# A recommender's attention over history: three gathers in 256 replaced by single-row DMAs from ScalarE's and SyncE's queues

## The chip, the cores and the metric

The kernel runs on one core of one Trainium2 chip. The metric is the device time of one execution in microseconds (us); lower is better. It is given as the median of several runs of the same program. One more execution is recorded by the hardware profiler; every row of a profile below comes from that one.

## The reference

For 16384 samples and a history of 200 items each, the reference looks up embedding rows of 64 floats, scores each history item against the sample's own item with a small two-layer network, sums the history with these scores, and passes the result through a head of three layers.

```python
it = i_emb[item]
h = i_emb[hist]                                   # 200 x 16384 rows of 64 floats
itb = jnp.broadcast_to(it[None], h.shape)
feat = jnp.concatenate([h, itb, h - itb, h * itb], axis=-1)
a = dice(feat @ au_W1 + au_b1, au_alpha, axis=1)  # mean and variance over the samples
w = a @ au_W2 + au_b2
cur = jnp.sum(w * jax.lax.stop_gradient(h), axis=0)
z = jnp.concatenate([u, it, c, cur], axis=-1)
z = dice(z @ W1 + b1, alpha1, axis=0)
z = dice(z @ W2 + b2, alpha2, axis=0)
return z @ W3 + b3
```

`dice(x)` is `x * (p + alpha * (1 - p))` with `p = sigmoid((x - mean) / sqrt(var + eps))`.

## The kernel before

**Setup.** A table in DRAM is built first: for every item its 64 floats and 64 more that are the part of the first layer that depends on the history item alone, 512 bytes a row. Meanwhile rows of item, user and category are gathered for the samples themselves. Then the head's weights are loaded (`load_head_weights`, L175), many small DMAs on SyncE's (SP's) queue.

**Main loop.** A step `k` handles 2048 history items: history row `k // 8`, chunk `k % 8` of the samples. A chunk is 16 tiles of 128 rows. There are 1600 steps: 7 turns of a hardware loop of 192 steps (24 history rows, L498) and 256 steps written out after it. Each step (`step`, L438) does a piece of several steps' work:

- `fetch(k)` (L366): GpSimd (POOL) issues 16 indirect DMAs (`gather`, L199, the instruction on L202), one for each tile; each fetches 128 table rows, one to a partition, into the buffer `land[k % 12]`. SP then loads `xit`, the part of the first layer that depends on the sample's item (L369).
- ScalarE (ACT) evaluates the sigmoid of step k-10 (L448) and scales it (L451), into the PSUM tile `pg`.
- VectorE (DVE) transposes step k-1's rows (`turn`, L377) into `hx`; ACT copies half of it to `ph` (L454); DVE adds the hidden layer of step k-2 (L390) and takes its statistics (L392); ACT copies `xit` to `px` (L458); DVE multiplies by the sample's item (L384) and TensorE (PE) adds the product's layer (L240).
- Once in 8 steps `moments` (L417) turns a history row's statistics into factors for the sigmoid; ACT takes the square root (L249).
- DVE weighs step k-10 (`weigh`, L396: L398 to L415) and adds it to `cur`.

`land` has 12 buffers. A buffer is used by a gather at step k, by the transpose at step k+1 and by `weigh` at step k+10, so POOL may run up to two steps ahead of DVE. The order inside an engine is the order written in `step`: the scheduler is switched off in this part.

**Synchronisation.** Each DMA sent from SP's or ACT's queue counts up one of eight semaphores, taken in turn in program order over both queues; a DMA waits until the earlier one on its semaphore has landed. POOL's DMAs have eight of their own.

**Head.** The last 10 steps are mixed with the first layer of the head (`layer1`, L527). Then come the factors of its normalisation (`row_factors`, L544), and for each of 8 chunks `dice` (L560: ACT L563, DVE L564 and L565), the second layer on PE (L593), the copy with bias by ACT (L595) and the sums by DVE (`row_sums`, L525). The third layer and the output follow.

Of the kernel before, what the change touches and what calls it, by code (L numbers as in the profile page):

```python
# [8 lines left out]
F32 = mybir.dt.float32  # L9
I32 = mybir.dt.int32  # L10
AF = mybir.ActivationFunctionType
# [3 lines left out]
P = 128  # L15
D = 64
# [3 lines left out]
CD = 2 * CH  # L20
LPB = 24
LAND = 12
EARLY = 4
IDX = 2
XI = 2
# [3 lines left out]
def din_kernel(  # L29
# [24 lines left out]
    nc = tc.nc  # L54
    L, B = r_hist.shape
    NT = B // P
# [51 lines left out]
    for g in range(2):  # L108
# [14 lines left out]

    land = [const.tile([P, TD, 2 * D], F32, name=f"land{i}") for i in range(EARLY)]
    idx = [const.tile([P, NT], I32, name=f"idx{i}") for i in range(IDX)]
    stats = [const.tile([P, 2 * ND, nc.vector.BN_STATS_DIM], F32, name=f"st{i}") for i in range(2)]
    rstds = [const.tile([P, 1], F32, name=f"rs{i}") for i in range(2)]
    shifts = [const.tile([P, 1], F32, name=f"sh{i}") for i in range(2)]
# [12 lines left out]
    J = P // (2 * ZB)  # L141
    w1a = const.tile([P, 4, P], F32, name="w1a")
    w1b = const.tile([P, 4, P + 2 * ZB * (J - 1)], F32, name="w1b")
    w2a = const.tile([P, 2 * Z2], F32, name="w2a")
    w2b = const.tile([P, J, 2 * Z2], F32, name="w2b")
    w3 = const.tile([2 * Z2, (2 * ND - 1) * 2 * ZO], F32, name="w3")

    za, zb, z2 = (
        [const.tile([n, 1], F32, name=f"{m}{i}") for i in ("b", "al", "1al")]
# [4 lines left out]
    mean_of = {  # L154
        n: const.tile([n * m, n * m], F32, name=f"mean{n}") for n, m in ((ZA, 2), (ZB, 2 * J), (Z2, 2))
    }
    zstats = [
        const.tile([n, m, nc.vector.BN_STATS_DIM], F32, name=f"zst{i}")
        for i, (n, m) in enumerate(((P, 2 * ND), (P, 2 * ND // J), (2 * Z2, 2 * ND)))
    ]  # L160
    zbase = dram.tile([ND + ND // J, P, CD], F32, name="zbase")

    for n, t in mean_of.items():
# [9 lines left out]
        nc.vector.tensor_scalar_mul(t, ph[: n * m, : n * m], 1.0 / m)  # L173

    def load_head_weights():  # L175
        for t in (w1a, w1b, w2a, w2b, w3):
            nc.vector.memset(t, 0.0)  # L177
        for g in range(2):
            for e in range(2):
                rows = W1.rearrange("(f d) z -> d f z", d=D)[e * S : (e + 1) * S]  # L180
                nc.sync.dma_start(w1a[quarter(e, g), :, ts(g, ZA)], rows[:, :, :ZA])
                z0 = 2 * ZB * (J - 1) + ZB * g
                nc.sync.dma_start(w1b[quarter(e, g), :, z0 : z0 + ZB], rows[:, :, ZA:])
            nc.sync.dma_start(w2a[ts(g, ZA), ts(g, Z2)], W2[:ZA])
            for j in range(J):
                nc.sync.dma_start(w2b[ts(2 * j + g, ZB), j, ts(g, Z2)], W2[ZA:])
            o0 = (ND - 1) * 2 * ZO + ZO * g
            nc.sync.dma_start(w3[ts(g, Z2), o0 : o0 + ZO], W3)
        nc.sync.dma_start(bias3, b3.partition_broadcast(S))
        for i, (v, w) in enumerate(((b1, b2), (alpha1, alpha2))):  # L190
            for g in range(2):
                nc.sync.dma_start(za[i][ts(g, ZA)], col(v)[:ZA])
                nc.sync.dma_start(z2[i][ts(g, Z2)], col(w))
            for m in range(2 * J):
                nc.sync.dma_start(zb[i][ts(m, ZB)], col(v)[ZA:])
        for t in (za, zb, z2):
            nc.vector.tensor_scalar(t[2], t[1], -1.0, 1.0, ALU.mult, ALU.add)

    def gather(dst, ids, rows):  # L199

        for n in range(ids.shape[1]):
            nc.gpsimd.indirect_dma_start(  # L202
                out=dst[:, n, :],
                out_offset=None,
                in_=rows,
                in_offset=bass.IndirectOffsetOnAxis(ap=ids[:, n : n + 1], axis=0),
            )
# [3 lines left out]

    def load_hist_ids(i, l):
        nc.sync.dma_start(idx[i], r_hist[ds(l, 1), :].rearrange("l (p n) -> p (l n)", n=NT))

    def by_tile(t, i):

# [118 lines left out]
    with ExitStack() as main:  # L335
# [19 lines left out]
        for i in range(2):  # L355
            nc.vector.memset(rstds[i], 0.0)
            nc.vector.memset(shifts[i], 0.0)
        nc.sync.dma_start(xit[-1 % XI], xi[ND - 1])

        def by_row(t):  # L360
            return t.rearrange("p (n d) -> p n d", d=D)
# [3 lines left out]

        def fetch(k):  # L366
            l, c = divmod(k, ND)
            gather(land[k % LAND], idx[l % IDX][:, ts(c, TD)], table)
            nc.sync.dma_start(xit[k % XI], xi[c])  # L369

        def turn(k):

# [65 lines left out]
        def step(k, last=None):  # L438


            def has(j):
                return last is None or j <= last

            if has(k):
                fetch(k)
            if has(k - 10):
                i = (k - 10) // ND % 2
                nc.scalar.activation(  # L448
                    by_row(pg), x_of(k - 10), AF.Sigmoid, bias=shifts[i], scale=rstds[i]
                )  # L450
                nc.scalar.activation(pg, pg, AF.Identity, bias=au_al, scale=au_1al)  # L451
            if has(k - 1):
                turn(k - 1)
                nc.scalar.copy(ph, hx[(k - 1) % 2][:, 0])  # L454
            if has(k - 2):
                hidden(k - 2)
            if has(k - 1):
                nc.scalar.copy(px, xit[(k - 1) % XI])  # L458
                product(k - 1)
            if has(k - 2) and (k - 2) % ND == ND - 1:  # L460
                moments((k - 2) // ND)
            if has(k - 10):
                weigh(k - 10)

        def fetch_ids(k, l0, n):
            l, c = divmod(k, ND)
            if c == 0 and l + 1 < n:
                load_hist_ids((l + 1) % IDX, l0 + l + 1)

        def window(j):  # L470
            return slice(2 * ZB * (J - 1 - j), 2 * ZB * (J - 1 - j) + P)

        def base_of_layer1():

            for rest in (False, True):
                for c in range(ND):
# [12 lines left out]
                    if last:  # L489
# [4 lines left out]
                        yield  # L494
                        yield

        rest_l = L % LPB + LPB
        with tc.For_i(0, L - rest_l, LPB) as l0:  # L498
            with tc.manual_schedule():
                for k in range(LPB * ND):  # L500
                    fetch_ids(k, l0, LPB + 1)
                    step(k)


# [11 lines left out]
        def rest_of(c):  # L516
            return home(homes[ND + c // J])
# [5 lines left out]
        def row_sums(i, n, m, t):  # L523
            for h in range(2):
                nc.vector.bn_stats(zstats[i][:, 2 * m + h, :], t[:n, ts(h, CH)])  # L525
# [34 lines left out]
        def dice(dst, t, p, factors, consts):  # L560
# [3 lines left out]
            nc.vector.tensor_scalar(p[:n], p[:n], consts[2], consts[1], ALU.mult, ALU.add)  # L564
            nc.vector.tensor_mul(dst[:n], p[:n], t)  # L565

        with tc.manual_schedule():
            work = base_of_layer1()
            for k in range(K):
                fetch_ids(k, L - rest_l, rest_l)  # L570
                step(k, last=K - 1)
                next(work, None)
            load_base(0, 1)
            for k in range(K, K + 10):
                step(k, last=K - 1)
                if k < K + 4:
                    load_base(*((2, 3), (ND, ND + 1), (4, 5), (6, 7))[k - K])
                c = k - K - 2
                if c >= 1:
                    keep1(c - 1)  # L580
                if c >= 0:
                    layer1(c)
            keep1(ND - 1)

            spare = [home(i) for i in range(18, 24)]
            fa, fb = row_factors(0, ZA, P), row_factors(1, ZB, P)
            for c in range(ND):
                if c % J == 0:
                    dice(rest_of(c), rest_of(c), spare[4 + c // J], fb, zb)
                a = spare[c % 4]  # L590
                dice(a, z_of(c), a, fa, za)
                po = (px, pz, pg, ph)[c % 4]
                layer(po[: 2 * Z2], [(w2a, a), (w2b[:, c % J], rest_of(c))])  # L593
                t = home(10 + c)[: 2 * Z2]
                nc.scalar.activation(t, po[: 2 * Z2], AF.Identity, bias=z2[0])  # L595
                row_sums(2, 2 * Z2, c, t)
            f2 = row_factors(2, Z2, 2 * Z2)
            n = ND * 2 * ZO
            for c in range(ND):
                a = spare[c % 4]  # L600
                dice(a, home(10 + c)[: 2 * Z2], a, f2, z2)
                at = (ND - 1 - c) * 2 * ZO
                for i in range(2):
                    nc.tensor.matmul(  # L604
                        px[:n, ts(i, CH)], w3[:, at : at + n], a[: 2 * Z2, ts(i, CH)],
                        start=(c == 0), stop=(c == ND - 1),
                    )
# [45 lines left out]
```

## Time and profile before

| What | Value |
|---|---|
| Timed runs, median of 3 | 36744.62 us (36743.43 to 36755.11) |
| Profiled execution | 32783.09 us |
| its span, first to last instruction | 32780.9 us |
| granted TensorE clock, mean | 0.547 of full speed |
| POOL gathers from the table, L202 | 25600, mean 943 ns |
| all POOL indirect DMAs | 25984 |
| DVE busy | 25567.4 us (78%) |
| ACT busy | 7755.2 us (24%) |
| DMA moved over the span | 2667.86 MB, 1214773 packets, 81 GB/s |

The profiled execution is shorter than the timed runs by 12%, so a duration from a row belongs to the profiled execution, and a sum of rows is to be set against its time. In a row of costly groups stand the line, the engine, the operation with its output and inputs, the count, then busy time in us and mean ns of one, then the engine's idle time just ahead of these instructions and what ended most of it; "issue" means that the engine waited for nothing that the profile shows. In a row of the timeline stand the start and the duration in us, and in brackets the idle time ahead and its releaser. SPq and ACTq are the queues on which these engines send DMAs.

### The profile page before, as it was taken

What the parts mean: (1) busy time and instruction counts of PE and PEld (TensorE: products, weight loads), DVE (VectorE), ACT (ScalarE), POOL (GpSimd) and SP (SyncE); (2) the same over time, 40 slices, a digit from 0 to 9 for tenths busy, and PEclk for the clock granted to TensorE, in tenths of its full rate; (3) what the DMA queues carried; (4) which work ended last, traced back from release to release, by engine and by line L of the source; (5) the groups of instructions that cost most, each with busy time, mean ns of one, the idle gap of its engine ahead of it and who ended that gap; (6) DMA issues with size and microseconds to landing.
All of it is one profiled execution on the core that took longest, in us unless ns stands there. A gap on an engine that the chain in (4) does not pass through costs nothing. (4 is left out here: it accounts for less than half of the span.)

```text
span 32780.9 us, 100656 instructions
## 1 busy us (share of the span) xinstructions
PE 6366.6 (19%) x7006; PEld 2038.0 (6%) x7006; DVE 25567.4 (78%) x28797; ACT 7755.2 (24%) x7105; POOL 24515.6 (75%) x25991
## 2 busy tenths in 40 slices
PE   3111111111111111111111111111111112221112
PEld 0000000000000000000000000000000000000000
DVE  7777777777777777777777777777777777777777
ACT  1222222222222222222222222222222222222222
POOL 7777777777777777777777777777777777777775
PEclk5555555555555555555555555555555555555555
DMA  5222222222222222222222222222222223332222
GB/s 157 80 79 79 79 79 79 79 79 79 79 80 80 79 78 79 79 79 80 79 79 79 79 79 78 79 79 80 78 79 79 79 79 85 88 90 81 79 79 60
DMA packets 1214773, 2667.86 MB, mean 81 GB/s; under 512 B 551244, under 2 KB 577388, under 8 KB 1207916
## 3 DMA queue, kind: packets, MB, share of 16 engines
q0 software_dynamic: 831488, 1691.97, 19.6%
q1 hardware_dynamic: 372012, 906.09, 9.1%
q10 hardware_dynamic: 10560, 63.79, 0.5%
q14 instruction: 692, 5.67, 0.1%
q8 instruction: 21, 0.34, 0.0%
HBM read 2590.90 MB, written 69.16 MB: 81 GB/s over the span
## 5 line engine op out<-in xcount | busy, mean ns | idle before, releaser
L202 POOL DMA_INDIRECT land<-table,idx x25600 | 24152.2, 943 | 7872.6 <-issue 7703.8
L377 DVE STREAM_TRANSPOSE hx<-land 64x1024 f32<-64x1024 f32 x6404 | 7938.2, 1240 | 6360.3 <-DMA land<-table,idx 6218.5
L240 PE MATMUL px<-hx,blk_m 128*128 128x512 f32 x6408 | 5927.6, 1080 | 26007.0 <-DVE hx L384 25941.1
L448 ACT ACTIVATE pg<-land,sh,rs 128x1024 f32<-128x1024 f32 x1610 | 1943.8, 1207 | 12980.0 <-DVE cur L415 11593.3
L454 ACT COPY ph<-hx 128x1024 f32<-128x1024 f32 x1601 | 1627.6, 1017 | 10365.2 <-DVE hx L377 10362.2
L240 PEld LDWEIGHTS px<-hx,blk_m 128*128 128x128 f32 x6408 | 1880.1, 324 | 30022.8 <-issue 29846.4
L392 DVE BATCH_NORM_STATS2 st<-land 128x6 f32<-128x512 f32 x3204 | 2060.9, 685 | 55.0
L400 DVE STREAM_TRANSPOSE hx<-pg 128x1024 f32<-128x1024 f32 x1610 | 2011.7, 1250 | 55.2
L414 DVE TENSOR_TENSOR pg<-land,ph 128x1024 f32<-128x1024 f32 x1610 | 1977.8, 1228 | 55.0
L415 DVE TENSOR_TENSOR cur<-pg,cur 128x1024 f32<-128x1024 f32 x1610 | 1970.5, 1224 | 55.6
L402 DVE TENSOR_REDUCE r<-hx 128x32 f32<-128x1024 f32 x1610 | 1964.0, 1220 | 55.3
L390 DVE TENSOR_TENSOR land<-px,hx 128x1024 f32<-128x1024 f32 x1602 | 1961.6, 1224 | 49.5
L398 DVE TENSOR_TENSOR pg<-pg,land 128x1024 f32<-128x1024 f32 x1610 | 1968.8, 1223 | 2.7 <-ACT pg L451 2.5
L384 DVE TENSOR_TENSOR hx<-ph,itT 128x1024 f32<-128x1024 f32 x1601 | 1932.0, 1207 | 0.0
L451 ACT ACTIVATE pg<-pg,au_al,au_1al 128x1024 f32<-128x1024 f32 x1610 | 1895.0, 1177 | 54.3
L458 ACT COPY px<-xit 128x1024 f32<-128x1024 f32 x1601 | 1627.2, 1016 | 383.3 <-DVE land L390 381.1
L409 DVE SCALAR_TENSOR_TENSOR ph<-r,au_bias,r 64x16 f32<-64x16 f32 x3220 | 771.3, 240 | 114.8
L406 DVE COPY r<-r 64x32 f32<-64x32 f32 x1610 | 337.2, 209 | 55.0
L448 ACT ACT_TABLE_LOAD x209 | 268.1, 1283 | 452.6 <-DVE w1a L177 314.6
L249 ACT ACT_TABLE_LOAD x203 | 260.4, 1283 | 6.7 <-PE ph L555 3.2
L249 ACT ACTIVATE std<-var,eps 128x1 f32<-128x1 f32 x201 | 59.2, 295 | 475.2 <-DVE var L435 475.2
L425 DVE COPY other<-mv 32x2 f32<-32x2 f32 x804 | 155.6, 194 | 15.1
(122 smaller groups left out, 1885.8 us busy)
## 6 DMA issues: line engine op xcount, KB each, us to landing
xit<-xi SPq DMA_DIRECT2D x1601, 512.0 KB
land<-table,idx POOLq DMA_INDIRECT x25600
table<-tab ACTq DMA_DIRECT2D x48, 1024.0 KB
tab<-in_L_rec_i_emb SPq DMA_DIRECT2D x48, 512.0 KB
zt<-ucT SPq DMA_DIRECT2D x32, 512.0 KB
idx<-in_r_hist SPq DMA_DIRECT2D x200, 64.0 KB
ucT<-t ACTq DMA_DIRECT2D x16, 512.0 KB
zbase<-zt SPq DMA_DIRECT2D x10, 512.0 KB
```

The source lines that it names most:

```text
L202: nc.gpsimd.indirect_dma_start(out=dst[:, n, :], out_offset=None, in_=rows, in_offset=bass.IndirectOffsetOnAxis(ap=ids[:, n : n + 1], axis=0),
L240: nc.tensor.matmul(dst[:, cols], lhsT, rhs[:, cols], start=(j == 0 and not onto), stop=(j == len(pairs) - 1), skip_group_check=onto,)
L377: nc.vector.transpose(dst.rearrange("p s (n t) -> p n s t", t=S), rows[ts(i, D), :, :, e])
L384: nc.vector.tensor_mul(hm, ph, itT[:, k % ND])
L390: nc.vector.tensor_add(x_of(k), by_row(px), by_row(hx[k % 2][:, 1]))
L392: nc.vector.bn_stats(stats[l % 2][:, 2 * c + i, :], x_of(k)[:, ts(i, TD // 2)])
L398: nc.vector.tensor_mul(by_row(pg), by_row(pg), x_of(k))
L400: nc.vector.transpose(yT, pg)
L402: nc.vector.tensor_reduce(r, yT.rearrange("p (i n u) -> p i n u", i=2, u=S), mybir.AxisListType.X, ALU.add)
L414: nc.vector.tensor_mul(by_row(pg), rows, w.unsqueeze(2).to_broadcast([P, TD, D]))
L415: nc.vector.tensor_add(cur[:, ts(c, TD)], by_row(pg), cur[:, ts(c, TD)])
L448: nc.scalar.activation(by_row(pg), x_of(k - 10), AF.Sigmoid, bias=shifts[i], scale=rstds[i])
```

## The change

Every eighth step (k % 8 = 7) and every sixteenth (k % 16 = 11) the last of the 16 tiles is no longer gathered by POOL. Its 128 rows are fetched by 128 plain DMAs of one row each, whose source address is read from a register: for the first kind from ACT's queue, 16 in each of the 8 steps before, for the second from SP's queue, 8 in each of the 16 steps before. They go into a buffer of their own (`side`, two of each kind), and ACT copies it into `land` at the step concerned. The addresses are loaded from the history by SP six steps before the first row is sent, multiplied by 512 by DVE four steps before, and read into registers (16 or 8 at once) in each step ahead of its DMAs. Part of these DMAs is sent before the loop starts.

The load of `xit` moves from `fetch`, at the head of the step, to behind ACT's second copy and SP's and ACT's row DMAs. To make room in memory the weights of the head's second and third layers and the head's statistics live in `zt`, a buffer that is free by then, and are loaded 16 steps before the end. In the head, chunk c's copy and sums (`keep2`) come after the matmuls of chunk c+2 have been issued.

```diff
+SIDES = ((8, 7), (16, 11))
+EARLIER = 0
+ROW = 4 * 2 * D
...
+    side = [[const.tile([P, 2 * D], F32, name=f"side{q}{i}") for i in range(2)] for q in range(2)]
+    addr = [[const.tile([1, P], I32, name=f"addr{q}{i}") for i in range(2)] for q in range(2)]
...
+    def load_addresses(q, m, l):
+
+        n = SIDES[q][1] % ND * TD + TD - 1
+        ids = r_hist[ds(l, 1), :].rearrange("l (p n) -> l n p", n=NT)[:, n : n + 1]
+        with nc.allow_non_contiguous_dma(reason="one index of each partition"):
+            nc.sync.dma_start(addr[q][m % 2].unsqueeze(1), ids)
+
+    def to_addresses(q, m):
+
+        nc.vector.tensor_scalar_mul(addr[q][m % 2], addr[q][m % 2], ROW)
+
+    def side_of(k):
+
+        for q, (every, at) in enumerate(SIDES):
+            if k % every == at:
+                return q, k // every
+        return None
...
+        flat = table.rearrange("v d -> (v d)").bitcast(U8)
+
+        queues = ((nc.scalar, mybir.EngineType.Activation), (nc.sync, mybir.EngineType.SP))
+
+        def rows_by_address(q, m, part):
+
+            dst = side[q][m % 2].bitcast(U8)
+            n = P // SIDES[q][0]
+            engine, kind = queues[q]
+            _, at = nc.values_load_multi_w_load_instructions(
+                addr[q][m % 2][:, ts(part, n)],
+                engines=(kind,), min_val=0, max_val=ROW * (V - 1),
+                skip_runtime_bounds_check_because="the DMA checks the address against the table",
+            )
+            for j, a in enumerate(at):
+                p = part * n + j
+                engine.dma_start(dst[p : p + 1], flat[ds(a, ROW)].rearrange("(o d) -> o d", o=1))
...
         def fetch(k):
             l, c = divmod(k, ND)
-            gather(land[k % LAND], idx[l % IDX][:, ts(c, TD)], table)
-            nc.sync.dma_start(xit[k % XI], xi[c])
+            n = TD - (side_of(k) is not None)
+            gather(land[k % LAND][:, :n], idx[l % IDX][:, c * TD : c * TD + n], table)
...
                 moments((k - 2) // ND)
+            if has(k):
+                if side_of(k):
+                    q, m = side_of(k)
+                    nc.scalar.copy(land[k % LAND][:, TD - 1], side[q][m % 2])
+                for q in (1, 0):
+                    every, at = SIDES[q]
+
+                    m, part = divmod(k + every + EARLIER - at, every)
+                    if has(m * every + at):
+                        rows_by_address(q, m, part)
+                nc.sync.dma_start(xit[k % XI], xi[k % ND])
             if has(k - 10):
                 weigh(k - 10)
...
+        for q, (every, at) in enumerate(SIDES):
+            done = divmod(every + EARLIER - at, every)
+            for m in range(done[0] + 1):
+                load_addresses(q, m, (m * every + at) // ND)
+                to_addresses(q, m)
+            for m in range(done[0] + 1):
+                for part in range(every if m < done[0] else done[1]):
+                    rows_by_address(q, m, part)
...
             for k in range(K):
+                if k == K - 2 * ND:
+                    load_late_weights()
                 fetch_ids(k, L - rest_l, rest_l)
...
-            for c in range(ND):
+            def activated(c):
                 if c % J == 0:
                     dice(rest_of(c), rest_of(c), spare[4 + c // J], fb, zb)
                 a = spare[c % 4]
                 dice(a, z_of(c), a, fa, za)
...
+            for c in range(ND + 2):
+                if c < ND:
+                    activated(c)
+                if c >= 2:
+                    keep2(c - 2)
             f2 = row_factors(2, Z2, 2 * Z2)
```

`fetch_ids` calls `load_addresses` and `to_addresses` at the steps named above. `load_late_weights` clears half of `zt` on DVE and loads the second and third layers' weights with 12 small DMAs on SP's queue.

More of the change, by code (lines that the diff above doesn't have):

```diff
@@ L22 @@
 LAND = 12
+SIDES = ((8, 7), (16, 11))
+EARLIER = 0
+ROW = 4 * 2 * D
+U8 = mybir.dt.uint8
 EARLY = 4
@@ L143, in din_kernel @@
     w1b = const.tile([P, 4, P + 2 * ZB * (J - 1)], F32, name="w1b")
-    w2a = const.tile([P, 2 * Z2], F32, name="w2a")
-    w2b = const.tile([P, J, 2 * Z2], F32, name="w2b")
-    w3 = const.tile([2 * Z2, (2 * ND - 1) * 2 * ZO], F32, name="w3")
     za, zb, z2 = (
@@ L156, in din_kernel @@
     }
[L157 to L160, printed above, removed]
     zbase = dram.tile([ND + ND // J, P, CD], F32, name="zbase")
@@ L175, in load_head_weights @@
     def load_head_weights():
-        for t in (w1a, w1b, w2a, w2b, w3):
+        for t in (w1a, w1b):
             nc.vector.memset(t, 0.0)
@@ L183, in load_head_weights @@
                 nc.sync.dma_start(w1b[quarter(e, g), :, z0 : z0 + ZB], rows[:, :, ZA:])
[L184 to L188, printed above, removed]
         nc.sync.dma_start(bias3, b3.partition_broadcast(S))
@@ L468, in fetch_ids @@
                 load_hist_ids((l + 1) % IDX, l0 + l + 1)
+            for q, (every, at) in enumerate(SIDES):
+                for ahead, make in ((6, True), (4, False)):
+                    m, part = divmod(k + every + EARLIER - at + ahead, every)
+                    row = (m * every + at) // ND
+                    if part == 0 and row < n:
+                        if make:
+                            load_addresses(q, m, l0 + row)
+                        else:
+                            to_addresses(q, m)
         def window(j):
@@ L495, in base_of_layer1 @@
                         yield
+        for q, (every, at) in enumerate(SIDES):
+            done = divmod(every + EARLIER - at, every)
+            for m in range(done[0] + 1):
+                load_addresses(q, m, (m * every + at) // ND)
+                to_addresses(q, m)
+            for m in range(done[0] + 1):
+                for part in range(every if m < done[0] else done[1]):
+                    rows_by_address(q, m, part)
         rest_l = L % LPB + LPB
@@ L500, in din_kernel @@
                 for k in range(LPB * ND):
-                    fetch_ids(k, l0, LPB + 1)
+                    fetch_ids(k, l0, LPB + 4)
                     step(k)
@@ L565, in dice, with load_late_weights @@
             nc.vector.tensor_mul(dst[:n], p[:n], t)
+        w2a = zt[:, 1, : 2 * Z2]
+        w2b = zt[:, 1, 2 * Z2 : 2 * Z2 * (J + 1)].rearrange("p (j z) -> p j z", j=J)
+        w3 = zt[: 2 * Z2, 1, 2 * Z2 * (J + 1) :]
+        zstats, n = [], 0
+        for rows, m in ((P, 2 * ND), (P, 2 * ND // J), (2 * Z2, 2 * ND)):
+            w = m * nc.vector.BN_STATS_DIM
+            zstats.append(zt[:rows, 0, n : n + w].rearrange("p (c s) -> p c s", c=m))
+            n += w
+        def load_late_weights():
+            nc.vector.memset(zt[:, 1], 0.0)
+            for g in range(2):
+                nc.sync.dma_start(w2a[ts(g, ZA), ts(g, Z2)], W2[:ZA])
+                for j in range(J):
+                    nc.sync.dma_start(w2b[ts(2 * j + g, ZB), j, ts(g, Z2)], W2[ZA:])
+                o0 = (ND - 1) * 2 * ZO + ZO * g
+                nc.sync.dma_start(w3[ts(g, Z2), o0 : o0 + ZO], W3)
         with tc.manual_schedule():
@@ L591, in din_kernel, with keep2 @@
                 dice(a, z_of(c), a, fa, za)
-                po = (px, pz, pg, ph)[c % 4]
-                layer(po[: 2 * Z2], [(w2a, a), (w2b[:, c % J], rest_of(c))])
+                layer(
+                    (px, pz, pg, ph)[c % 4][: 2 * Z2], [(w2a, a), (w2b[:, c % J], rest_of(c))]
+                )
+            def keep2(c):
                 t = home(10 + c)[: 2 * Z2]
-                nc.scalar.activation(t, po[: 2 * Z2], AF.Identity, bias=z2[0])
+                nc.scalar.activation(
+                    t, (px, pz, pg, ph)[c % 4][: 2 * Z2], AF.Identity, bias=z2[0]
+                )
                 row_sums(2, 2 * Z2, c, t)
+            for c in range(ND + 2):
[3 more added lines that the diff above has]
+                    keep2(c - 2)
             f2 = row_factors(2, Z2, 2 * Z2)
```

## The prediction

> **What bounds the kernel now.** I read the page first: busy shares and costliest groups.
>
> ```profile
> PE 6366.6 (19%) x7006; PEld 2038.0 (6%) x7006; DVE 25567.4 (78%) x28797; ACT 7755.2 (24%) x7105; POOL 24515.6 (75%) x25991
> ...
> L202 POOL DMA_INDIRECT land<-table,idx x25600 | 24152.2, 943 | 7872.6 <-issue 7703.8
> L377 DVE STREAM_TRANSPOSE hx<-land 64x1024 f32<-64x1024 f32 x6404 | 7938.2, 1240 | 6360.3 <-DMA land<-table,idx 6218.5
> ```
>
> DVE has the larger busy share, yet it is not the bound. POOL's idle time before its gathers is nearly all "issue": nothing that the profile shows holds it. DVE's idle time (6360 us) ends with a gather landing. So POOL is never kept waiting, and DVE waits for POOL. The timeline of one step in the middle of the run shows the two clocks (start, duration, instruction, idle before it):
>
> ```profile
> 9999.44 0.94 POOL L202 DMA_INDIRECT land<-table,idx  x1 [0.30 <-issue]
> 10000.27 1.21 ACT L448 ACTIVATE pg<-land,sh,rs 128x1024 f32<-128x1024 f32 x1 [8.39 <-DVE cur L415]
> 10000.69 0.94 POOL L202 DMA_INDIRECT land<-table,idx  x1 [0.30 <-issue]
> 10001.52 1.18 ACT L451 ACTIVATE pg<-pg,au_al,au_1al 128x1024 f32<-128x1024 f32 x1
> ...
> 10004.59 5.00 DVE L377 STREAM_TRANSPOSE hx<-land 64x1024 f32<-64x1024 f32 x4 [4.35 <-DMA land<-table,idx]
> ...
> 10009.62 1.02 ACT L454 COPY ph<-hx 128x1024 f32<-128x1024 f32 x1 [6.93 <-DVE hx L377]
> ...
> 10010.87 1.02 ACT L458 COPY px<-xit 128x1024 f32<-128x1024 f32 x1 [0.24 <-DVE land L390]
> ...
> 10011.92 0.32 SPq L369 DMA_DIRECT2D xit<-xi  x1
> ...
> 10020.28 1.21 ACT L448 ACTIVATE pg<-land,sh,rs 128x1024 f32<-128x1024 f32 x1 [8.39 <-DVE cur L415]
> ```
>
> A gather starts every 0.94 + 0.30 us; the count by windows gives 4001 POOL instructions in 5000 us, so 1.2497 us each, and 16 make a step of 20.0 us. DVE's own work in a step is 15.65 us and it idles 4.35. ACT works 1.21 + 1.18 + 1.02 + 1.02 = 4.4 us, waits 0.24 inside, and is free in two stretches: 8.39 us after L458 and 6.93 us after L451. The second stretch counts too: if L448 and L451 come late, only DVE's L398 needs them, and that stands behind the copies. So ACT can take some 15.3 us more per step before it delays DVE, and DVE has 4.35 us itself. SP sends one large DMA per step, 0.32 us.
>
> [...] the trace has DMA engines 29% busy by windows. [...] 0.94 us of POOL for a gather, 0.32 us of SP for an issue. [...] A row DMA is 1x512 bytes[...]. No run before shows such a DMA. [...]
>
> **Part 1, gathers removed.** Of 1600 steps, 200 have k%8 = 7 and 100 have k%16 = 11; each loses one of its 16 gathers. 300 x 1.2497 = 375 us off POOL in the profiled execution. All of it is on the path, since POOL waits for nobody. What is late next: the average step becomes 20.0 x 253/256 = 19.77 us, still far over DVE's 15.65 (about 18.3 in the one step of 8 that makes moments).
>
> The profiled execution took 32783.1 us (span 32780.9 and 2.2 around it), the median of the timed runs is 36744.6, 12% more. The profile cannot say where those 3961 us are. If POOL's pitch is longer there, it is 3961 / 25984 gathers = 0.152 us each, pitch 1.402, and the gain 300 x 1.402 = 421 us. If they are fixed, it is 375. I take 421: so much time must repeat with the steps, and POOL is the engine that sets the step.
>
> **Part 2, rows on ACT.** Every step adds one register load of 16 addresses and 16 row DMAs behind L458. For a small hardware DMA the nearest row is SP's loads of bias pieces in the setup:
>
> ```profile
> 508.16 3.55 SPq L195 DMA_DIRECT2D zbb<-in_L_rec_b  x8
> ```
>
> Eight in 3.55 us: 0.445 us each, though each is sent with eight completion semaphores going round. 16 x 0.445 = 7.1 us. [...] I take 2. Waits: ACT and SP share the eight semaphores, so in the half of the block where both send, each has four in turn. A load lands within 1.96 us (ids issued at 7.87, POOL starts on it at 9.83), so four take at least 2.4 us and not 1.8: 1.2 us for eight. Block: 7.1 + 2 + 1.2 = 10.3 us, against 15.3 free. [...] Queued behind it are L448 and L451; they come 10.3 - 8.39 = 2 us later, inside the 6.93 that follow. Cost 0. If that cover goes, each us over 15.3 first eats DVE's 4.35 and then lengthens all 1600 steps. Once in 8 steps ACT also copies side to land, 128x128, under 0.3 us and a step ahead of the transpose that reads it: 0.
>
> **Part 3, rows on SP, and what is moved past them.** 8 x 0.445 + 2 = 5.6 us of 20 on a queue that is otherwise asleep. The load of xit, formerly ahead of everything, now stands behind SP's rows, which share semaphores with ACT's; it starts up to about 10 us after L458 instead of at once, and its reader is the next L458, 20 us later. Cost 0. The load of the next idx waits for the row before to be gathered, and SP's rows wait behind it; that release comes about 6 us before ACT's block of that step. 0. The address loads (six steps ahead) and DVE's scaling of 128 numbers (four ahead, about 0.2 us, 300 times) hide in DVE's 4.35 us: 0.
>
> **Part 4, DMA engines.** [...] A mean packet now costs 0.29 x 16 x 32781 / 1214773 = 0.125 us[...]. [...] Gathers may land a little later, which DVE's slack takes. Bound: 0 to +100 us. I take 0.
>
> **Part 5, start.** Before the loop SP now sends 40 row DMAs and 5 loads, 40 x 0.445 + 5 x 2 = 28 us, less about 6 us of weights that move to the end. SP enters the loop 22 us later than at 519; the load of xit[0] comes at about 547, while step 1 wanted it landed at 546. I take 10 us, bounds 0 and 30.
>
> **Part 6, head.** The chain of waits has one entry per chunk of the second layer:
>
> ```profile
> 32665.57 5.86 PE pz L240 x8
> 32675.90 5.37 PE pg L240 x8
> 32685.79 5.97 PE ph L240 x8
> ```
>
> 5.9 us of PE every 10.2 us: between them ACT's L595, the next L563 and DVE's two operations run one after another. With reading and writing two chunks apart PE has the next chunk ready, and the stretch from 32649.7 to 32738.8 (89.1 us, PE busy 47.3) becomes lead-in 5.4 + 47.3 + last activation and sums 2.4 = 55. Gain 34; bounds 20 and 38. The late weights load while gathers still run: 0.
>
> **Sum.** Profiled: 32783 - 375 + 10 - 34 = 32384. Timed: 36744.6 - 421 + 10 - 34 = 36300.
>
> **Rivals.** (a) *ACT becomes the bound, slower.* A row DMA with a register address and checked bounds may cost more than a plain one. ACT then goes 4.65 + load + 16 x row per step, and overtakes POOL's 20.0 us with a row over (20.0 - 4.65 - 2) / 16 = 0.83 us (0.98 if the timed step is 22.4). [...] about 39100. For it: no row DMA of this form was seen. Against: 0.445 would have to double. (b) *The pitch of the gathers grows* with the traffic of small pieces: 15 ns on 25300 gathers gives back 380 us; about 36700, no change. Against: the pitch is 1.25 both in the setup, with table loads beside it, and in the loop. (c) *Partial*: fixed 375, a late ACT in the steps with moments, a start of 30: 36380 to 36670. That the change removes fewer gathers than it says is excluded: the loop body issues 36 fewer in 192 steps and the remainder 48, and 7 x 36 + 48 = 300.
>
> **How the numbers follow.** Forecast 0.70 (36240 to 36380), partial 0.10, no change 0.04, slower 0.16. The bound for "same" is 0.2%, about what a measurement of this kernel can tell from no change. The range 36240 to 36680 holds the first two, 0.80. Faster 0.80, same 0.04, slower 0.16.
>
> **What would show it.** Right: 25300 gathers at 943 ns and 0.30 idle by issue; DVE's wait for gathers shrinks by about 0.2 us a step; ACT's wait for DVE cur gone or small, its wait for DVE hx cut to about 5 us; about 55 us for the head's second layer. Wrong: POOL idle released by DVE instead of issue, DVE waiting for ACT pg, or gathers over 1.26 us apart.

## The result, and the profile after

| | Median | Lowest to highest | Ratio to the kernel before |
|---|---|---|---|
| before | 36748.33 us | 36743.43 to 36755.11, 4 runs | 1 |
| after | 40716.01 us | 40672.31 to 40854.62, 4 runs | 1.1086, 95% interval 1.1059 to 1.1113 |

The change costs 3968 us; the forecast was a gain of 444. The chips come in two sorts: on some the kernel before takes 32.78 ms, on others 36.7 to 36.9 ms, three of each among the six used for the experiments. So every time below is compared with runs of the kernel before on the same chip. The profile of before in the first part is of the first sort, the timed runs there and here are of the second. I call them 32.8 chips and 36.7 chips. Each chip of the experiments was used on one occasion only, so whether a chip always belongs to its sort is not shown.

The profiled execution of after (40672.31 us) is of a 36.7 chip. From its page, the span and the costliest groups:

```profile
span 40670.5 us, 181533 instructions
...
L197 POOL DMA_INDIRECT land<-table,idx x25300 | 23930.2, 946 | 15963.7 <-issue 15722.4
...
L414 DVE TENSOR_TENSOR hx<-ph,itT 128x1024 f32<-128x1024 f32 x1601 | 1950.5, 1218 | 14112.3 <-ACT ph L484 8840.7
L407 DVE STREAM_TRANSPOSE hx<-land 64x1024 f32<-64x1024 f32 x6404 | 7919.9, 1237 | 132.0 <-DMA land<-table,idx 40.2
L478 ACT ACTIVATE pg<-land,sh,rs 128x1024 f32<-128x1024 f32 x1610 | 1944.3, 1208 | 27155.0 <-DMA side<-table 10364.0
```

The gathers are as long as before (946 ns), but POOL's idle time has doubled. DVE no longer waits for gathers: 132 us against 6360. It waits 14,112 us at L414, for ACT's copies, scaled sigmoid and what stands before them. One stretch of the timeline shows how (start, duration, instruction, idle before it and its releaser; the first line is from the view of ACT alone):

```profile
19976.41 32.92 ACTq L388 DMA_DIRECT2D side<-table  x15
...
20003.12 0.94 POOL L197 DMA_INDIRECT land<-table,idx  x1 [0.30 <-issue]
20004.37 0.95 POOL L197 DMA_INDIRECT land<-table,idx  x1 [0.30 <-issue]
20010.16 1.21 ACT L478 ACTIVATE pg<-land,sh,rs 128x1024 f32<-128x1024 f32 x1 [32.74 <-DMA side<-table]
...
20012.51 1.01 ACT L484 COPY ph<-hx 128x1024 f32<-128x1024 f32 x1
...
20013.54 1.23 DVE L414 TENSOR_TENSOR hx<-ph,itT 128x1024 f32<-128x1024 f32 x1 [21.38 <-ACT ph L484]
20013.59 8.54 ACTq L388 DMA_DIRECT2D side<-table  x14
...
20019.24 1.23 DVE L444 TENSOR_TENSOR pg<-land,ph 128x1024 f32<-128x1024 f32 x1
...
20021.23 0.95 POOL L197 DMA_INDIRECT land<-table,idx  x1 [15.92 <-issue]
```

ACT stands for 32.74 us before its sigmoid, because the rows are ahead of it in its queue; DVE stands still for 21.38 us; no buffer comes free, and POOL stands still for 15.92 us (the page says "issue", but POOL goes on 0.76 us after DVE's last reading of the buffer, L444, has ended at 20020.47). The first line against the 14 rows after L484 shows the size of the trouble: 15 rows in 32.92 us, then 14 rows in 8.54.

What stretches the rows is seen in the single instructions of the trace. ACT has 25,603 register moves in it, median 29 ns; 4800 of them last 680 to 720 ns, as do 5277 of its DMAs and 4666 of SP's moves. From 19983 to 20009 us nearly every start and every end of an instruction on ACT falls on a step of 0.70 us, 1.40 us for each instruction when ACT alone is busy; where SP sends too, the two take turns. In other stretches a row (a move and a DMA) takes 0.32 us.

The same kernel on a 32.8 chip takes 32358.75 us, a gain of 428. From the page of that run (`e18_after4` below):

```profile
span 32357.4 us, 181533 instructions
...
L197 POOL DMA_INDIRECT land<-table,idx x25300 | 23873.8, 944 | 7776.5 <-issue 7380.3
...
L407 DVE STREAM_TRANSPOSE hx<-land 64x1024 f32<-64x1024 f32 x6404 | 7926.4, 1238 | 2173.5 <-DMA land<-table,idx 1973.4
...
L414 DVE TENSOR_TENSOR hx<-ph,itT 128x1024 f32<-128x1024 f32 x1601 | 1934.8, 1208 | 3849.2 <-ACT ph L484 3849.2
```

The same 181,533 instructions, and POOL is the bound as before: its idle time is 25,300 times 0.31 us, nearly all of it issue. Not one of ACT's 25,603 moves there lasts 680 to 720 ns.

### The profile page after: what moved, and what is told of

The parts are those of the page before. It is cut to its first block, busy times and chain, and to the rows that moved or that the text cites. A ratio compares the mean times of both kernels' runs of the same rounds, so it can differ in the third digit from the quotient of the medians.

```text
span 40670.5 us, 181533 instructions
## 1 busy us (share of the span) xinstructions
PE 6362.5 (16%) x7006; PEld 2038.5 (5%) x7006; DVE 25514.1 (63%) x29095; ACT 7640.8 (19%) x7405; POOL 24294.5 (60%) x25691
## 3 DMA queue, kind: packets, MB, share of 16 engines
q10 hardware_dynamic: 61760, 77.00, 0.5%
## 5 line engine op out<-in xcount | busy, mean ns | idle before, releaser
L414 DVE TENSOR_TENSOR hx<-ph,itT 128x1024 f32<-128x1024 f32 x1601 | 1950.5, 1218 | 14112.3 <-ACT ph L484 8840.7
L407 DVE STREAM_TRANSPOSE hx<-land 64x1024 f32<-64x1024 f32 x6404 | 7919.9, 1237 | 132.0 <-DMA land<-table,idx 40.2
L444 DVE TENSOR_TENSOR pg<-land,ph 128x1024 f32<-128x1024 f32 x1610 | 1977.8, 1228 | 64.8 <-DVE ph L439 5.7
L484 ACT COPY ph<-hx 128x1024 f32<-128x1024 f32 x1601 | 1614.9, 1009 | 587.6 <-DVE hx L407 567.4
L236 DVE STREAM_TRANSPOSE rT<-tab 64x512 f32<-64x512 f32 (+1 forms) x196 | 138.0, 704 | 58.1 <-issue 38.7
L197 POOL DMA_INDIRECT land<-in_L_rec_u_emb,ids x128 | 121.1, 946 | 72.4 <-issue 37.8
```

The costliest lines, as they stand in the source:

```text
L197: nc.gpsimd.indirect_dma_start(out=dst[:, n, :], out_offset=None, in_=rows, in_offset=bass.IndirectOffsetOnAxis(ap=ids[:, n : n + 1], axis=0),
L407: nc.vector.transpose(dst.rearrange("p s (n t) -> p n s t", t=S), rows[ts(i, D), :, :, e])
L414: nc.vector.tensor_mul(hm, ph, itT[:, k % ND])
L444: nc.vector.tensor_mul(by_row(pg), rows, w.unsqueeze(2).to_broadcast([P, TD, D]))
```

## The experiments

The theories, as the expectations use them. **A**: the rows of the two queues hold each other up. **B**: a row DMA on ACT's queue is dear by itself, whatever SP does. **D**: the loss belongs to the 36.7 chips, where instructions start and end in steps of 0.70 us, and the change adds 81,000 instructions. Kernels in one table ran on the same chip. In kernels with edits the line numbers move a little; the tiles tell which line is which.

### First chip: 32.8

before: 32784.84 us.

`e0_before`, no edit. 

> The kernel before, unchanged, to see why its profiled execution (32783 us) and its timed runs (36745 us) differ. If the extra 12% is longer gathers, POOL's pitch is about 1.40 us in this profile; if it is stretches in which an engine holds POOL up, the pitch stays 1.25 and POOL's idle time has another releaser; if the profiled execution is simply another state, this one may again show 32.8 ms.

`e2_left_out`: the 300 tiles are neither gathered nor fetched (they stay zero, so a part of the history is left out); the rest of the change is kept.

```diff
-                        rows_by_address(q, m, part)
+                        pass
```

> After, with the row DMAs, register loads and addresses left out: in the 300 steps concerned the last tile is not fetched at all and a buffer of zeros is copied in its place, so 1 tile in 85 of the work is wrong data. Measures what removing 300 gathers is worth by itself, with the head's change. If POOL sets the step also in the timed runs: 36745 - 421 - 34 = 36290, or 32783 - 375 - 34 = 32374 in the other state. If something else sets it there: about 36700.

`e3_act_only`: rows on ACT's queue only, and only those tiles taken from POOL.

```diff
-SIDES = ((8, 7), (16, 11))
+SIDES = ((8, 7),)
...
-                for q in (1, 0):
+                for q in (0,):
```

> After with ACT's rows alone (one tile in every 8 steps); SP sends no rows and the tile of every sixteenth step goes back to POOL. Theory A (the two queues hold each other up, as the 0.70 us steps in which ACT and SP alternate suggest): ACT's block falls from up to 35 us to about 8 us and the time is at or below that of before, about 36450. Theory B (a row DMA on ACT is dear whatever SP does): the slowdown stays, about 39500 to 40700.

`e4_sp_only`: rows on SP's queue only.

```diff
-            if k % every == at:
+            if q == 1 and k % every == at:
...
-                for q in (1, 0):
+                for q in (1,):
...
```

> After with SP's rows alone (one tile in every 16 steps); ACT sends none and the tile of every eighth step goes back to POOL. Theory A and theory B both: near the time of before, 36600, since SP's queue holds nothing but loads that are needed a step later. [...]

| Kernel | Time, us | Ratio | Interval |
|---|---|---|---|
| e0_before | 32789.32 | one run | |
| e2_left_out | 32343.52 | 0.9865 | 0.9849 to 0.9882 |
| e3_act_only | 32475.91 | 0.9906 | 0.9889 to 0.9922 |
| e4_sp_only | 32604.17 | 0.9945 | 0.9928 to 0.9962 |

Here the rows cost next to nothing. Rows on ACT gain 309 us, on SP 181 (the gain of the head is in both); leaving the tiles out gains 441, and the whole change will gain 428 on the sixth chip. So B falls, as a rule for every chip. That these gains stand beside a loss of 3968 us says that the chip matters, and A stays open.

### Second chip: 36.7

before: 36763.97 us.

`e5_after`, no edit. 

> The kernel after, unchanged. Before has now run at 32785 us on this chip where the first comparison had 36748; ACT's rows alone gave 32476, SP's alone 32604. Theory A (the two queues disturb each other only when both send rows): slow here too, 36000 or more, with ACT's and SP's register moves at 0.70 us. Theory D (the slowness came with the chip or state in which before took 36.7 ms): the two gains add up, 32785 - 309 - 181 plus the head's change counted twice, about 32330.

`e1_no_rows`: all 16 tiles gathered, no row DMAs; the moved load of `xit`, the late weights and the head two chunks apart are kept.

```diff
-SIDES = ((8, 7), (16, 11))
+SIDES = ()
...
-                for q in (1, 0):
+                for q in ():
```

> After with no tile moved at all: 16 gathers in every step, no row DMAs, no addresses; what stays is the later load of xit, the late weights and the head's second layer two chunks apart. Both theories: 32785 - 34 = 32750; a start shorter by some 6 us of weights may add.

| Kernel | Time, us | Ratio | Interval |
|---|---|---|---|
| e5_after | 40657.52 | 1.1056 | 1.1038 to 1.1074 |
| e1_no_rows | 36713.02 | 0.9986 | 0.9979 to 0.9993 |

The rows make the whole loss. The profile of `e1_no_rows` is also the only one of a kernel close to before on a 36.7 chip (100,656 instructions, as many as before):

```profile
L197 POOL DMA_INDIRECT land<-table,idx x25600 | 24155.4, 944 | 11780.4 <-issue 11547.3
...
L407 DVE STREAM_TRANSPOSE hx<-land 64x1024 f32<-64x1024 f32 x6404 | 7920.7, 1237 | 1669.5 <-issue 1585.6
...
L444 DVE TENSOR_TENSOR pg<-land,ph 128x1024 f32<-128x1024 f32 x1610 | 1978.4, 1229 | 1397.4 <-issue 1363.8
...
L439 DVE SCALAR_TENSOR_TENSOR ph<-r,au_bias,r 64x16 f32<-64x16 f32 x3220 | 778.5, 242 | 2272.9 <-issue 1933.8
```

and its timeline of DVE:

```profile
20011.95 0.23 DVE L439 SCALAR_TENSOR_TENSOR ph<-r,au_bias,r 64x16 f32<-64x16 f32 x1 [0.47 <-issue]
20014.04 0.24 DVE L439 SCALAR_TENSOR_TENSOR ph<-r,au_bias,r 64x16 f32<-64x16 f32 x1 [1.86 <-issue]
20015.44 1.23 DVE L444 TENSOR_TENSOR pg<-land,ph 128x1024 f32<-128x1024 f32 x1 [1.16 <-issue]
...
20021.04 1.24 DVE L407 STREAM_TRANSPOSE hx<-land 64x1024 f32<-64x1024 f32 x1 [0.16 <-issue]
20022.44 1.24 DVE L407 STREAM_TRANSPOSE hx<-land 64x1024 f32<-64x1024 f32 x1 [0.16 <-issue]
20023.84 1.23 DVE L420 TENSOR_TENSOR land<-px,hx 128x1024 f32<-128x1024 f32 x1 [0.16 <-issue]
```

Starts lie 2.09 us, then 1.40 us apart, multiples of 0.70, and the idle time before them has no releaser. DVE itself goes in the steps here, and it has no slack. POOL's gathers are still 1.249 us apart (median); what lengthens the run is some 880 pauses: POOL's idle time before its gathers is 11,780 us here and was 7873, so 3908 us more. Mean pitch: 1.402 us.

### Third chip: 36.9

before: 36904.21 us.

`e7_after2`, no edit. 

> The change again, unaltered, for a chip on which the kernel before takes 32.78 ms. Theory D (the loss belongs to the condition in which the kernel before takes 36.7 ms, and instructions are let through on steps of 0.70 us): there 32,784 - 309 - 181 = about 32,300 us, the gains of the two queues alone added up, and no step of 0.70 us in the trace; where the kernel before takes 36.7 ms, 40,660 us again. Theory A (the two queues hold each other up, in any condition): 34,000 us or more even where the kernel before takes 32.78 ms.

`e8_act_only2`, the edit of e3. 

> Only the rows on ScalarE's queue, 16 a step, none on SyncE's. Where the kernel before takes 36.7 ms: theory A, in which only both queues together are dear, 36,500 us or less, the gain of the gathers left out (1.0 %) kept; theory D, in which each instruction added costs a share of one stream, two thirds of the loss of 3,950 us, so about 39,300 us. Where it takes 32.78 ms: 32,476 us again by both.

`e9_static_rows`: one DMA per row, at a fixed address (other rows than asked for are fetched), so without register load and moves.

```diff
-            _, at = nc.values_load_multi_w_load_instructions(
...
-            for j, a in enumerate(at):
+            for j in range(n):
                 p = part * n + j
-                engine.dma_start(dst[p : p + 1], flat[ds(a, ROW)].rearrange("(o d) -> o d", o=1))
+                engine.dma_start(dst[p : p + 1], flat[ds(p * ROW, ROW)].rearrange("(o d) -> o d", o=1))
```

> Each row still a DMA of its own on the same queue, but at an address known when the program is built, so that the register load and the register move ahead of each row are gone (the rows fetched are then others than the ids ask for). Where the kernel before takes 36.7 ms: if the number of instructions sets the loss, half of them are gone and the loss falls from 3,950 us to about 1,900 us, 38,600 us; if the DMA itself is dear, it stays at 40,600 us. Where the kernel before takes 32.78 ms: 32,300 us.

`e10_one_dma`: the rows of a step and queue in one DMA, again at a fixed address.

```diff
+            p = part * n
+            engine.dma_start(dst[p : p + n], flat[ds(p * ROW, n * ROW)].rearrange("(o d) -> o d", o=n))
```

> The 16 rows of a step on ScalarE's queue as one DMA of 16 rows at a fixed address, and the 8 on SyncE's likewise: the same bytes, the same rows' worth of packets, and 78,000 instructions fewer (the rows fetched are then others than the ids ask for). Where the kernel before takes 36.7 ms: if instructions set the loss, it is gone, and the time is 36,300 to 36,700 us; if the transfers do, 40,000 us or more. Where the kernel before takes 32.78 ms: 32,300 us.

| Kernel | Time, us | Ratio | Interval | ACT instructions added per step |
|---|---|---|---|---|
| e7_after2 | 40641.42 | 1.1002 | 1.0983 to 1.1020 | 33 |
| e8_act_only2 | 42087.74 | 1.1404 | 1.1379 to 1.1429 | 33 |
| e9_static_rows | 37478.08 | 1.0157 | 1.0140 to 1.0174 | 16 |
| e10_one_dma | 36778.81 | 0.9967 | 0.9955 to 0.9980 | 1 |

The bytes and packets of the rows are the same in the first, third and fourth (61,760 packets on ACT's queue in each), though the third and fourth read the same 128 rows of the table again and again. With 1 instruction per step the loss is gone, with 16 it is small, with 33 it is there, and it grows faster than the count: e9 has half of the row instructions and lost 574 us where about 1,900 was expected. So the transfers are not the cause. `e8_act_only2` is a miss for every theory. A expected a gain; D expected 39,300; it came out dearer than both queues together. A is finished with it. Why 12,800 row DMAs fewer on SP make it slower is not settled.

### Fourth chip: 32.8

before: 32786.54 us.

`e11_dots`: no rows (the 300 tiles stay zero); instead 32 copies of one number on ACT in each step.

```diff
-                        rows_by_address(q, m, part)
+                for j in range(32):
+                    nc.scalar.copy(dots[:, j : j + 1], dots[:, 32 + j : 33 + j])
```

> No row is fetched at all (the tiles beside the gathers stay zero, so 3 gathers of 16 steps are left out and not made up for); in the place of each step's rows ScalarE does 32 copies of one number, the same count of instructions as the 16 moves and 16 DMAs of the change, without a DMA, a register or a semaphore of another queue. Where the kernel before takes 36.7 to 36.9 ms: if any instruction of ScalarE is let through on the steps of 0.70 us while the gathers run, the time is near the change's, 40,000 us or more; if only what its sequencer does (register moves, DMA issues, semaphore waits) is, the copies take about 0.2 us each, 6.4 us a step in ScalarE's 15 us of free time, and the time is that of the kernel with neither, about 36,400 to 36,800 us. Where the kernel before takes 32.78 ms: 32,340 us.

`e12_half`: half as many rows.

```diff
-SIDES = ((8, 7), (16, 11))
+SIDES = ((16, 7), (32, 11))
```

> The change with half as many rows: one tile in 16 steps on ScalarE's queue and one in 32 on SyncE's, so 8 and 4 rows a step, each with its move and its DMA. That is as many instructions a step on the two queues as the kernel with static rows had (24), in half as many DMAs. Where the kernel before takes 36.7 to 36.9 ms: if the number of instructions sets the loss, about what static rows gave, a ratio of 1.016; if the moves and the register load are dear in themselves, half of the change's loss, 1.05; Where the kernel before takes 32.78 ms: 32,784 - 245 = 32,540 us.

`e13_no_gathers`: the loop's gathers are left out, so only the tiles fetched by row are there.

```diff
+            if n < 0:
                 gather(land[k % LAND][:, :n], idx[l % IDX][:, c * TD : c * TD + n], table)
```

> The change without the 15 or 16 gathers of each step (all the tiles but those fetched by row stay zero), the rows and all else kept. VectorE's 15.7 us a step are then the longest work, so some 25,500 to 27,000 us. If the steps of 0.70 us come from the gathers that run beside, they are gone from the trace in every condition, and a row's move and DMA take 0.32 us throughout; if the rows make them by themselves, they stay, the rows of a step take 20 us and more, and the time is above 33,000 us where the kernel before takes 36.7 ms.

`e14_sp_only2`, the edit of e4. 

> Only the rows on SyncE's queue, 8 a step, none on ScalarE's; nothing that computes waits behind them. Where the kernel before takes 36.7 to 36.9 ms: if the loss comes through ScalarE's queue, where the sigmoid stands behind the rows, it is gone, and the time is 36,500 to 36,800 us; if any instruction added takes its part of one stream, a third of the change's loss or more, above 37,800 us. Where it takes 32.78 ms: 32,604 us again.

| Kernel | Time, us | Ratio | Interval |
|---|---|---|---|
| e11_dots | 32342.65 | 0.9865 | 0.9848 to 0.9881 |
| e12_half | 32565.88 | 0.9933 | 0.9916 to 0.9949 |
| e13_no_gathers | 26254.29 | 0.8008 | 0.7994 to 0.8021 |
| e14_sp_only2 | 32606.32 | 0.9945 | 0.9929 to 0.9962 |

On this chip these could not tell the theories apart. They do show that 32 copies cost nothing there (32,342.65 us; `e2_left_out` took 32,343.52), that both queues together are no trouble at half the rows, and that all but the gathers takes 26,254 us.

### Fifth chip: 36.7

before: 36760.47 us.

`e15_after3`, no edit. 

> The change unaltered once more. Where the kernel before takes 32.78 ms: the two halves alone gave 309 and 178 us, so if they add up, 32,300 us; if the two queues hold each other up whatever the condition, 34,000 us or more. Where the kernel before takes 36.7 to 36.9 ms: 40,650 us again.

`e16_dots2`, the edit of e11. 

> The 32 copies of one number on ScalarE in each step again, in the place of the rows (no rows fetched at all; the tiles beside the gathers stay zero), for the condition in which the kernel before takes 36.7 to 36.9 ms: if any instruction of ScalarE is let through on steps of 0.70 us while the gathers run, near the change's time, 40,000 us or more; if only what its sequencer does for moves, DMA issues and semaphores is, 36,400 to 36,800 us. Where the kernel before takes 32.78 ms: 32,342 us again.

| Kernel | Time, us | Ratio | Interval |
|---|---|---|---|
| e15_after3 | 40712.52 | 1.1070 | 1.1051 to 1.1088 |
| e16_dots2 | 40335.32 | 1.0974 | 1.0956 to 1.0993 |

`e16_dots2` is the run that decides. Without a row DMA, a register or a wait on another queue, 32 tiny copies on ACT cost 3575 us, nine tenths of the 3952 that the change costs on this chip. Their group in the page of `e11_dots` (32.8 chip) and then of `e16_dots2`, with DVE's wait:

```profile
L486 ACT COPY dots<-dots 1x1 f32<-1x1 f32 x51200 | 4895.2, 185 | 0.0
```

```profile
L486 ACT COPY dots<-dots 1x1 f32<-1x1 f32 x51200 | 6335.8, 187 | 15058.3 <-issue 14383.7
...
L403 DVE TENSOR_TENSOR hx<-ph,itT 128x1024 f32<-128x1024 f32 x1601 | 1943.7, 1214 | 13796.2 <-ACT ph L473 13091.2
```

A copy lasts 185 or 187 ns, and copies overlap (12 in 1.36 us below); the second kernel has 15,058 us of idle time before copies, and nearly all of it waits for nothing that the profile shows. The timeline of `e16_dots2`:

```profile
20004.63 1.36 ACT L486 COPY dots<-dots 1x1 f32<-1x1 f32 x12
...
20007.20 0.19 ACT L486 COPY dots<-dots 1x1 f32<-1x1 f32 x1 [1.21 <-issue]
...
20008.60 0.19 ACT L486 COPY dots<-dots 1x1 f32<-1x1 f32 x1 [1.21 <-issue]
...
20010.00 0.19 ACT L486 COPY dots<-dots 1x1 f32<-1x1 f32 x1 [1.21 <-issue]
...
20046.87 1.23 DVE L403 TENSOR_TENSOR hx<-ph,itT 128x1024 f32<-128x1024 f32 x1 [25.64 <-ACT ph L473]
20047.71 2.41 ACT L486 COPY dots<-dots 1x1 f32<-1x1 f32 x25
```

Twelve copies in 1.36 us, then one every 1.40, then 25 in 2.41 us. The change between the two goes with POOL. Over the whole trace of `e16_dots2`, the share of copies that start 0.69 us or more after the copy before (the first copy of a step is left out):

| Time since POOL's run of gathers began, or ended | Copies | Share at 0.69 us or more |
|---|---|---|
| 0 to 4 us after it began | 615 | 22% |
| 4 to 12 us | 14295 | 5% |
| 12 to 16 us | 2420 | 27% |
| 16 to 20 us | 506 | 87% |
| 20 to 25 us | 3340 | 17% |
| 25 to 30 us | 2144 | 67% |
| 30 to 40 us | 4014 | 84% |
| 40 to 60 us, still running | 4924 | 99% |
| 0 to 3 us after it ended | 299 | 71% |
| 3 to 5 us | 415 | 53% |
| 5 to 7 us | 1267 | 9% |
| 7 to 20 us | 14632 | under 1% |

(A run is broken where two gathers start over 2 us apart.) So the steps are rare in the first 12 us of a run, the rule past 30 us, and gone some 7 us after the gathers stop; between 12 and 30 us the share goes up and down (17% at 20 to 25 us). The time since the last pause is not the whole rule: in `e1_no_rows` POOL's runs last 18.7 us in the median, with pauses of some 4.5 us beyond the pitch, and DVE is in steps in the first 8 us of a run too (50 to 70% of the instructions on six of its lines start over 0.1 us after the one before has ended).

The head has no gathers, and it is a second sign. From the first matmul of its statistics (L612, `ph<-zmv,mean`) to the end, `after` and `e1_no_rows` take 86.2 and 86.4 us on 36.7 chips, `e18_after4` and `e2_left_out` 86.0 and 86.6 on 32.8 chips, and more than 15 us after the last gather no register move, wait or DMA of an engine lasts 680 to 720 ns. Yet the program has 3.9 instructions per us from 20 us after the last gather on, more than the 2.7 of `e1_no_rows` as a whole. Both signs tie the steps to the gathers in time; that the gathers cause them is not shown, since a kernel without gathers was measured on a 32.8 chip alone.

### Sixth chip: 32.8

before: 32786.42 us.

`e17_sp_only3`, the edit of e4. 

> Only the rows on SyncE's queue, 8 a step, none on ScalarE's. Where the kernel before takes 36.7 to 36.9 ms: if the loss comes through ScalarE's order, in which sigmoid and copies stand behind the rows, it is gone, and the time is 36,500 to 36,800 us; if any instruction added on any queue takes its part of one stream, a third of the change's loss or more, above 37,800 us. Where it takes 32.78 ms: 32,605 us again.

`e18_after4`, no edit. 

> The change unaltered. Where the kernel before takes 32.78 ms: the two halves alone gave 309 and 178 us, so if they add up, 32,300 us; if the two queues together are too much whatever the condition, 34,000 us or more. Where the kernel before takes 36.7 to 36.9 ms: 40,650 to 40,710 us again.

| Kernel | Time, us | Ratio | Interval |
|---|---|---|---|
| e17_sp_only3 | 32605.95 | 0.9945 | 0.9928 to 0.9962 |
| e18_after4 | 32358.75 | 0.9869 | 0.9853 to 0.9886 |

The change itself gains 1.3% on a 32.8 chip. Whether rows on SP alone cost anything on a 36.7 chip was not measured: all three runs of that edit fell on 32.8 chips.

## Why the prediction was wrong

**Two steps failed,** and both carried a wait from the profile of a 32.8 chip to a 36.7 chip: the gain of 421 us in Part 1 was not there, and the cost 0 of Part 2 was the loss, since the block of ACT's rows took 22.7 us in the median and not 10.3, over the 15.3 held to be free.

**Part 1, gain 421.** "The profile cannot say where those 3961 us are ... I take 421: so much time must repeat with the steps, and POOL is the engine that sets the step." The 3961 us were the other sort of chip, and there POOL does not set the step. The mean pitch of 1.402 us that I worked out is what `e1_no_rows` has, but it is 1.249 us and pauses. DVE, whose instructions start 1.40 or 2.09 us apart there, makes them. With POOL no longer the bound, 300 gathers fewer are worth little: `e10_one_dma` gains 125 us, of which some 51 are the rest of the change (`e1_no_rows` gains 51), so about 75 and not 421, less what its own two DMAs a step cost.

**Part 2, cost 0.** The block of ACT's rows, from the register load to the last DMA, is 9.84 us in the median on the 32.8 chip (10.3 predicted): a register load of 1.19 us (2 taken, a guess for which no trace had a number), 0.32 us a row (0.445 taken), and some 3.5 us of waits (1.2 taken). On the 36.7 chip it is 22.7 us in the median, over the 15.3. The cover I named was gone, and then the loop's steps grew longer, as the text said they would. DVE's slack, which was to give way first, was not there either (`e1_no_rows`). The mean pitch of after's gathers is 1.575 us, the median 1.252: 25300 x 1.575 - 25600 x 1.402 = 3956 us, against a loss of 3968. So nearly all of the loss is pauses of POOL, and DVE's 14,112 us at L414 say that they begin at ACT.

**Rival (a)** had the right place and, from prices that no trace had shown, a time not far off (39100 against 40716; it was given 0.16). The price is another: not a DMA that is dear for its form, since copies of one number do the same, but instructions that start and end in steps of 0.70 us. Nothing in a profile of a 32.8 chip shows that price.

**Part 3, cost 0.** The price was right (5.6 us predicted, 5.19 measured on the 32.8 chip), one wait was not. "That release comes about 6 us before ACT's block of that step" is wrong: once in 8 steps SP can send the next `idx` only some 31 us after ACT's block has begun. SP's rows stand behind it, and ACT's tenth row waits for one of them by a shared semaphore (from 20100.61 to 20130.73 in the trace), as the timeline of `e18_after4` shows:

```profile
20095.06 0.36 SPq L502 DMA_DIRECT2D xit<-xi  x1
...
20095.35 37.87 ACTq L388 DMA_DIRECT2D side<-table  x16
...
20126.41 0.36 SPq L208 DMA_DIRECT2D idx<-in_r_hist  x1
...
20136.96 1.23 DVE L414 TENSOR_TENSOR hx<-ph,itT 128x1024 f32<-128x1024 f32 x1 [21.70 <-ACT ph L484]
```

16 rows take 37.87 us there, and DVE stands for 21.70. POOL goes on through it on this chip, so it cost next to nothing: that Part 3 came out at 0 is luck. The same wait is in the trace of after (20.9 us from 20034.49). The copies, which have no such wait, made nine tenths of the loss without it; what it adds to the loss of the change itself was not measured.

**Part 4, DMA engines.** No trace of before had a row DMA, so the cost of 0 was an estimate. ACT's queue before and after:

```profile
q10 hardware_dynamic: 10560, 63.79, 0.5%
```

```profile
q10 hardware_dynamic: 61760, 77.00, 0.5%
```

51,200 packets and 13.21 MB more for 25,600 rows: two packets and 516 bytes a row, in the trace of after one of 512 B and one of 4 B, 25,600 more of each, so no row was split. The packets of the queue take 0.5% of the 16 engines' span in both. Nor are the gathers longer beside the rows: 943 ns in before, 944 in `e18_after4`. The cost of 0 stands.

**Parts 5 and 6, and the sum.** Start: POOL has 378 instructions between 520 and 1000 us on the 32.8 chip as before, and 3200 up to 5000 us against 3199, so 0 and not 10. Head: the second layer now lies without gaps. Its first matmuls and what follows its last, before and then in `e18_after4`:

```profile
32655.15 1.99 PE L240 MATMUL px<-land,w2a 128*80 128x512 f32 x2 [7.00 <-DVE land L565]
...
32739.54 0.27 PE L550 MATMUL ph<-zmv,mean 80*80 80x1 f32 x2 [3.23 <-DVE zmv L548]
```

```profile
32282.75 6.09 PE L253 MATMUL px<-land,zt 128*80 128x512 f32 x8 [7.00 <-DVE land L627]
32288.67 3.60 PE L253 MATMUL pz<-land,zt 128*80 128x512 f32 x8
...
32309.27 3.60 PE L253 MATMUL ph<-land,zt 128*80 128x512 f32 x8
32316.10 0.40 PE L612 MATMUL ph<-zmv,mean 80*80 80x1 f32 x2 [3.23 <-DVE zmv L610]
```

From the first matmul to L612 it takes 33.4 us, against 84.4 to L550 before: 51 us gained, 34 predicted. The other 17 are shorter matmuls, PE's busy time there being 30.1 us and not 47.3: eight matmuls take 3.4 us in place of 5.9, and the granted clock is 0.90 in this stretch and was 0.68. The profiled sum was 375 - 10 + 34 = a gain of 399; the 32.8 chip gives 428, and 375 + 51 - 0 is 426. DVE's idle time at L407 and L414 together fell by 338 us, 0.21 a step; 0.2 was predicted. The sum was near for the chip of the profile, with a start and a head that were off and a wait that POOL's lead hid. The forecast was for the other.

## What to carry to other kernels

When the profiled execution and the timed runs differ by 12%, the profile may not be of what is timed: a bound read in it is not to be carried over untested, and a sum should be made for each possible bound. A change that spreads work over idle queues adds instructions; ask what it costs if each takes 1.40 us, as in the steps here, and not only the 0.03 to 0.2 us that the profile of a 32.8 chip shows, and what stands behind them in the same queue. Tiny copies put where the work would go price the instructions alone, before any of the work is written.

## What the runs showed of the hardware

- On 36.7 chips, instructions on ACT and SP (`after`) and on DVE (`e1_no_rows`) go in steps of 0.70 us (a start and an end, 1.40 us for one) in stretches of the loop while POOL gathers. 99% of ACT's copies in `e16_dots2` start 0.69 us or more after the one before once POOL has gathered for 40 us without a pause. In the head of `after`, more than 15 us after the last gather, no move, wait or DMA lasts 680 to 720 ns, and on a 32.8 chip (`e18_after4`) not one of ACT's moves does. 32 copies of 0.19 us in each step of the loop cost 10% on a 36.7 chip (1.0974) and nothing on a 32.8 chip (32,342.65 us against 32,343.52 without).
- What makes the steps is open. The mean rate of instructions does not tell: `e18_after4` has 2 x 181,533 / 32,357 = 11.2 starts and ends per us on a 32.8 chip, where ACT's moves show no step; on 36.7 chips the head of `after` has none at 3.9 instructions per us, and `e1_no_rows` has steps at 2.7. Each timed run here has its span and granted clock from a recording, so whether the loss would be there without one is not known.
- Also open: why rows on ACT alone cost more (1.140) than with SP's rows beside them (1.100, same chip).
- Of the kernels that do the whole work, the change is the fastest on a 32.8 chip (0.987). On a 36.7 chip, of those measured, only its other half is worth keeping (`e1_no_rows`, 0.9986: the head two chunks apart, the later load of `xit` and the late weights). No version with rows was found that gains on both; half the rows and rows on SP alone were not measured on a 36.7 chip.
